# Reordering the end of layer 1: placing masks, products of blocks 6 and 7, chosen rows and block 7's scaling

## Chip, cores, metric

The kernel runs on one NeuronCore of a Trainium2 chip. The metric is device time in microseconds (us) of one execution; lower is better. A core has five engines that run side by side, each working through its own queue in program order: PE (TensorE, matrix products and transposes), VectorE (DVE in the profile), ScalarE (ACT), GpSimd (POOL) and SyncE (SP, which issues transfers). An engine stops at an instruction whose input isn't there yet, and all that stands behind it in the same queue waits too.

## What is computed

Four layers, each an attention part and a feed-forward part on a residual x, 4096 tokens of 128 values in fp32. The change is in the feed-forward part of the second layer (layer 1 in the code):

```
def _ln(x, g, b):
    mu = jnp.mean(x, axis=-1, keepdims=True)
    var = jnp.mean(jnp.square(x - mu), axis=-1, keepdims=True)
    return (x - mu) * jax.lax.rsqrt(var + EPS) * g + b
...
x1 = jnp.einsum('btd,hd->bth', x, sw1) + sb1
x2 = jnp.einsum('btd,hd->bth', x, sw2) + sb2
sh = _ln(jax.nn.silu(x1) * x2, s_ln_g, s_ln_b)
shared_out = jnp.einsum('bth,dh->btd', sh, sw3) + sb3
x_moe = x[index_b, index_t]
shared_scores = jax.nn.sigmoid(x_moe @ sg_w.T + sg_b)
expert_scores = jax.nn.sigmoid(x_moe @ eg_w.T + eg_b)
top1_idx = jnp.argmax(expert_scores + exp_bias, axis=-1)
...
shared_moe_out = shared_out[index_b, index_t] * shared_w[:, None]
h1 = jnp.einsum('md,ehd->meh', x_moe, ew1) + eb1
h2 = jnp.einsum('md,ehd->meh', x_moe, ew2) + eb2
z = _ln(jax.nn.silu(h1) * h2, sel_ln_g, sel_ln_b)
...
final_out = shared_out.at[index_b, index_t].set(shared_moe_out + expert_moe_out)
```

Every token takes a shared path with 64 hidden values. 256 chosen tokens take one of eight experts as well, and their result replaces that of the shared path. The input of both is the layer-normed residual, and the result is added to the residual. What follows is layer 2's attention, which starts with a norm of the new residual.

## The kernel before

**Blocks.** The 4096 tokens are eight blocks of 512 (`TB`), each held as four tiles of 128 tokens by 128 values (`x[b]`, `J` = 4). The order of the work is written out by hand (`tc.manual_schedule`): the instructions of each engine stand in the order of the calls. Layer 1 runs a loop of stages over the blocks with fixed lags, and then a list of calls for what remains of the last blocks: that list is what the change edits.

**A block's shared path.** `f_stats`, `f_scale` and `f_turn` norm a block, write its rows to DRAM (`by_rows`, issued by SP) and transpose it. `f_product(b)` makes the 128 products per token on PE and starts a tanh on ScalarE; the function it leaves in `t[b]["gated"]` makes silu times product on VectorE (L916, L919). `z_stats` takes mean and variance on VectorE (L715, L717, L718), with the inverse root on GpSimd (L242, L243, L720). `z_scale` scales four tiles of 128x64 on ScalarE (L726), `z_turn` transposes them on PE and evicts on ScalarE (L946) into one of two buffers `zts`. `z_out` makes the output product and adds it on VectorE (L790); `z_out_by_three` has ScalarE scale it (L970) and GpSimd add it (L973), the addition being returned to be called later (`add2`, `add3`, ...).

**The chosen rows.** `chosen_rows` gathers 256 rows from `by_rows` by two indirect transfers of GpSimd (L987), which need all row writes landed. `chosen_products` transposes them (L995), and makes gates, both hidden layers of all experts and the shared products; `chosen_gates` finds the expert; `chosen_select` and `chosen_shared` make z for the chosen expert and for the shared path; `chosen_norm` and `chosen_scale` norm it (znc, L726); `chosen_mix` makes the weights (L1071 to L1081); `chosen_affine`, `chosen_turn`, `chosen_shared_out`, `chosen_products_out` and `chosen_out` make the 256 result rows `val`. For block 0 they are put in by a product with 0/1 masks: `put_rows` makes the masks on GpSimd (L772), `chosen_put_product` multiplies, `chosen_put` adds to `x[0]`. For the other blocks `chosen_back` writes the rows to DRAM (`back`, L1151), whence layer 2 fetches them.

**The end.** Block 0's new residual is normed (`stats_of`, `scaled`), transposed (L748), and evicted (L750) as layer 2's first `xt`. Layer 2's first steps are `qb` on VectorE (L2086), the products for q and k on PE, and q's eviction with `qb` on ScalarE (L1441). `keep_clock(4)` before the last transposes makes four products of the unit matrix with itself whose result isn't used.

Of the kernel before, what the change touches and what calls it, by code (L numbers as in the profile page):

```python
# [160 lines left out]
def body(ctx, tc, dram, spans, x_in, ib, it, ic, ei, out):  # L161
# [23 lines left out]
    def bank(tag="one"):  # L185
        if tag == "one" and "own" in banks:
            return banks["own"]
        return banks["pool"].tile([P, TB], F32, tag=tag, name="ps1", bufs=banks["tags"][tag])
# [579 lines left out]
    def put_rows(b, pool, engine, tag=None):  # L768

        put = pool.tile([P, 4 if tag else 2, TB], F32, tag=tag or "put", name="put")  # L770
        for m in range(2):
            engine.tensor_scalar(  # L772
                put[:, m, :], c["iota512"], float(b * TB), at_col[:, m : m + 1], ALU.add, ALU.is_equal
            )
        return put

    def keep_clock(n):

        ps = bank()
        for _ in range(n):  # L780
            mm(cols(ps, 0), ident, ident)
# [12 lines left out]
    def layer1():  # L794
# [9 lines left out]
        with tc.tile_pool(name="l1", bufs=2) as wp, tc.tile_pool(name="l1c", bufs=1) as once:  # L804
# [102 lines left out]
            def f_turn(b):  # L907
                t[b]["fxt"] = turned(wp, "fxt", t[b]["fxn"], 5)
# [22 lines left out]
            def f_gate(b):  # L931
                f_product(b)
                t[b]["gated"]()

            def z_stats(b):
                t[b]["zby"] = stats_of(t[b]["z"], J)

            def z_scale(b):
                t[b]["zn"] = wp.tile([P, J, 64], F32, tag="zn", name="zn")
                scaled(t[b]["zn"], t[b]["z"], t[b]["zby"], J)  # L940

            def z_turned(zn, i, n):
                ps = bank()
                for j in range(n):
                    nc.tensor.transpose(ps[:64, j * P : (j + 1) * P], zn[:, j, :], ident)
                nc.scalar.activation(  # L946
                    zts[i][:64, : n * P],
                    ps[:64, : n * P],
                    AF.Identity,
                    bias=l1["slb"][:64],  # L950
                    scale=l1["slg"][:64],
                )

            def z_turn(b):
                z_turned(t[b]["zn"], b % 2, J)

            def z_out(b):
                zt = zts[b % 2]
# [3 lines left out]
            def z_out_by_three(b):  # L962


                zt = zts[b % 2]
                pv = by_token([(lambda j: cols(zt, j), l1["sw3"][:65])], None)
                zo = wp.tile([P, J, D], F32, tag="zo", name="zo")
                for j in range(J):
                    k = b * J + j
                    nc.scalar.activation(  # L970
                        zo[:, j, :], pv[:, j, :], AF.Identity, scale=rest[:, k : k + 1]
                    )
                return lambda: nc.gpsimd.tensor_tensor(x[b], x[b], zo, ALU.add)  # L973
# [73 lines left out]
            def chosen_shared():  # L1047
                c_["gated"]()
# [14 lines left out]
            def chosen_norm():  # L1063

                c_["by"] = stats_of(c_["zs"], 4)
# [17 lines left out]
            def chosen_scale():  # L1083
                c_["zn"] = zn = once.tile([P, 4, 64], F32, tag="znc", name="znc")
                scaled(zn, c_["zs"], c_["by"], 4)
# [8 lines left out]
                        (ALU.mult, ALU.add)[k],  # L1094
                    )

            def chosen_turn():
                zn = c_["zn"]
                z_turned(zn[:, 2:, :], 2, 2)
                pts = c_["pts"] = []  # L1100
                for m in range(2):
                    ze = wp.tile([P, 8, 64], F32, tag="ze", name="ze")
                    nc.vector.tensor_tensor(
                        ze,
                        zn[:, m, :].unsqueeze(1).to_broadcast([P, 8, 64]),
                        c_["pick"][:, m, :].unsqueeze(2).to_broadcast([P, 8, 64]),
                        ALU.mult,
                    )
                    pt = bank()
                    zf = ze.rearrange("p (i e) h -> p i (e h)", i=4)  # L1110
                    for i in range(4):
                        nc.tensor.transpose(cols(pt, i), zf[:, i, :], ident)
                    zte = wp.tile([P, TB], F32, tag="zte", name="zte")
                    (nc.vector.tensor_copy if m else nc.scalar.copy)(zte, pt)
                    pts.append(zte)
# [39 lines left out]
            def chosen_put_product():  # L1155
                c_["pv"] = put_product(c_["put"])
# [26 lines left out]
            with tc.manual_schedule():  # L1183

                nc.scalar.activation(
                    stat.tile([P, J], F32, tag="nb", name="nb")[:, :1], half[:, :1], AF.Exp
                )
                for zt in zts:
                    nc.gpsimd.memset(zt[64:65, :], 1.0)
                nc.gpsimd.memset(top_row, 0.0)  # L1190
                nc.gpsimd.memset(top_row[:1, :], 1.0)
                for k, name in enumerate(("eb1", "eb2")):
                    lo, hi = spans["rows"][name]
                    nc.sync.dma_start(ebs[:, k, :], dram["rows"][:, lo:hi].partition_broadcast(P))
                nought = once.tile([P, J, D], F32, tag="nought", name="nought")
                nc.gpsimd.memset(nought, 0.0)
                for b in range(1, NB):
                    nc.sync.dma_start(
                        back[b * TB : (b + 1) * TB, :].rearrange("(j p) d -> p j d", p=P), nought
                    )  # L1200
                for i in range(NB):
                    for f, lag in stages:
                        if 0 <= i + lag < NB and (f, i) != (turn_, 0):
                            f(i + lag)


                gather(7)
                f_stats(5)
                output(6)
                z_scale(1)  # L1210
                attend(7)
                f_stats(6)
                f_gate(2)
                turn_o(7)
                f_scale(5)
                z_turn(1)
                output(7)
                f_stats(7)
                f_scale(6)
                f_turn(5)  # L1220
                f_scale(7)
                z_out(1)
                z_stats(2)
                c_["put"] = put_rows(0, wp, nc.gpsimd)
                chosen_rows()
                chosen_biases()
                f_turn(6)
                f_gate(3)
                z_scale(2)
                z_stats(3)  # L1230
                f_turn(7)
                z_turn(2)
                f_gate(4)
                z_stats(4)
                chosen_products()
                chosen_gates()
                z_scale(3)
                add2 = z_out_by_three(2)
                f_product(5)
                chosen_select()  # L1240
                z_turn(3)
                add3 = z_out_by_three(3)
                chosen_shared()
                chosen_norm()
                add2()
                z_scale(4)
                z_turn(4)
                add3()
                chosen_scale()
                t[5]["gated"]()  # L1250
                z_stats(5)
                chosen_mix()
                add4 = z_out_by_three(4)
                f_product(6)
                chosen_affine()
                chosen_turn()
                add4()
                chosen_shared_out()
                t[6]["gated"]()
                chosen_products_out()  # L1260
                z_stats(6)
                z_scale(5)
                z_turn(5)
                f_product(7)
                chosen_out()
                chosen_put_product()
                z_scale(6)
                add5 = z_out_by_three(5)
                t[7]["gated"]()
                z_stats(7)  # L1270
                chosen_put()

                by = stats_of(x[0], J)
                chosen_back()
                add5()
                z_turn(6)
                z_scale(7)
                z_out(6)
                z_turn(7)
                xn = norm.tile([P, J, D], F32, tag="xn", name="xn")  # L1280
                scaled(xn, x[0], by, J)
                nc.gpsimd.tensor_tensor(
                    x[0], x[0], bc["lb"].unsqueeze(1).to_broadcast([P, J, D]), ALU.add
                )
                z_out(7)
                keep_clock(4)
                t[0]["next"] = turned(norm, "xt", xn)


    I3 = 352  # L1290
# [861 lines left out]
```

## Time and profile before

| | us |
|---|---|
| runs of the kernel | 1476.65, 1475.78, 1473.11 (median 1475.78) |
| profiled execution | 1477.4, of which span 1475.6 |
| PE busy | 1396.4 (95% of the span) |
| VectorE busy | 982.0 (67%) |
| ScalarE busy | 1047.2 (71%) |
| GpSimd busy | 652.3 (44%) |

"Busy" is the time in which an engine had an instruction under way. The list that the change edits covers some 480 to 533 us of the span, that is 3.6% of it. To read this stretch one needs the views by time: the chain of waits (the work that ended last, followed back from the end, here in order of time), the timeline of single instructions (start, length, engine, line, operation, output<-inputs, and in brackets how long the engine had been idle and what ended that), and the table of stretches (busy time of each engine and the TensorE clock that was granted, 1.00 being full speed).

| chosen steps before | starts at, us |
|---|---|
| first gather of chosen rows (GpSimd, L987) | 486.08 |
| scaling of the chosen rows' z (ScalarE, znc) | 507.85 |
| its transposes (PE, L945 on znc) | 513.84 |
| product with the masks (PE, val and put) | 520.61 |
| norm of block 0: scaling (ScalarE, xn) | 527.69 |
| eviction of layer 2's first xt (ScalarE, L750) | 532.51 |
| first q of layer 2 (ScalarE, L1441) | 536.97 |

### The profile page before, as it was taken

Reading aid. Unit: us, or ns where it says so; the run is one execution under the profiler, and the core shown is the slowest. Engines: PE = TensorE matmul, PEld = TensorE weight load, DVE = VectorE, ACT = ScalarE, POOL = GpSimd, SP = SyncE. Lnnn points to the kernel's source line nnn. Section 1 sums busy time; section 2 is a strip of 40 time slices with the busy share of each in tenths; the row PEclk is TensorE's granted clock in tenths of the full one; section 3 lists DMA queues with packets and bytes.
Section 4 is the critical chain, followed back from the end, with each engine's and each line's share of the span. In section 5 each row is a group of like instructions: output and inputs, shape, how many; then the busy total and the mean of one; then the engine's idle time right before and its main releaser. Section 6 shows DMA issues by size and latency. Waiting matters only on the chain.

```text
span 1475.6 us, 22195 instructions
## 1 busy us (share of the span) xinstructions
PE 1396.4 (95%) x7716; PEld 670.2 (45%) x7716; DVE 982.0 (67%) x2050; ACT 1047.2 (71%) x2140; POOL 652.3 (44%) x749
## 2 busy tenths in 40 slices
PE   7789999999889889999999999999999999999997
PEld 3652222222367554443443445444445454454465
DVE  6776665675377558642673487786786777877876
ACT  7869999999777556664865585876876867668632
POOL 6647666665555533310530172452442623524423
PEclk9999999999899889999999999999999999999998
DMA  4039999898431010101000000000000000000000
GB/s 170 1 54 132 134 129 130 129 128 114 103 132 30 18 40 24 36 3 29 1 1 1 1 1 8 1 1 8 1 1 8 1 8 1 1 8 1 1 8 15
DMA packets 33233, 59.42 MB, mean 40 GB/s; under 512 B 5602, under 2 KB 25634, under 8 KB 28643
## 3 DMA queue, kind: packets, MB, share of 16 engines
q1 hardware_dynamic: 32416, 56.18, 21.9%
q8 instruction: 61, 1.00, 0.3%
q10 hardware_dynamic: 578, 1.57, 0.3%
q14 instruction: 50, 0.40, 0.1%
q0 software_dynamic: 128, 0.26, 0.0%
HBM read 49.70 MB, written 8.29 MB: 39 GB/s over the span
## 4 chain that ended last, share of the span: by engine, by line
PE 69%; ACT 14%; DVE 9%; DMA 5%; issue 1%; POOL 1%; POOLq 0%; DVEq 0%; SPq 0%; ACTq 0%
PE ps L246 66%; ACT hm L563 6%; DMA gs<-gates 4%; ACT hm L562 3%; ACT ex L1469 2%; DMA gates<-eq 1%; DVE s L715 1%; DVE nm L1463 1%; ACT xn L1385 1%; PE ps L1799 1%; ACT xn L726 1%; POOL rs L243 0%; DVE pr L575 0%; ACT h L384 0%; DVE x L270 0%
## 5 line engine op out<-in xcount | busy, mean ns | idle before, releaser
L1469 ACT ACTIVATE ex<-ps,nm 128x512 f32<-128x512 f32 x512 | 346.3, 688 | 182.4 <-DVE nm L1463 176.3
L1463 DVE TENSOR_REDUCE nm<-ps 128x2 f32<-128x1024 f32 x256 | 300.5, 1216 | 61.3 <-PE ps L246 60.9
L246 PE MATMUL ps<-q,k 64*128 64x512 f32 x1024 | 256.9, 617 | 5.7 <-ACT ex L1469 4.9
L246 PE MATMUL ps<-ex,vs 128*64 128x512 f32 x1024 | 233.8, 598 | 0.0
L581 POOL TENSOR_TENSOR acc<-acc,pr 128x512 f32<-128x512 f32 x119 | 166.6, 1400 | 107.9 <-DVE pr L575 99.7
L1484 POOL TENSOR_TENSOR vs<-v,sm 128x256 f32<-128x256 f32 x128 | 81.4, 636 | 296.7 <-DVE sm L1483 267.6
L563 ACT ACTIVATE hm<-ps,blob_f 128x1536 f32<-128x1536 f32 x128 | 196.4, 1535 | 0.0
L246 PE MATMUL ps<-xt,blob_a 128*128 128x512 f32 x304 | 152.3, 627 | 0.7 <-ACT xt L750 0.7
L575 DVE SCALAR_TENSOR_TENSOR pr<-ps,blob_f,gs 128x512 f32<-128x512 f32 x120 | 90.1, 751 | 91.0 <-PE ps L246 74.6
L246 PE MATMUL ps<-h,w 32*128 32x512 f32 x1024 | 148.0, 639 | 2.3 <-ACT xt L750 0.8
L246 PEld LDWEIGHTS ps<-q,k 64*128 64x128 f32 x1024 | 87.0, 185 | 137.5 <-issue 69.9
L246 PE MATMUL ps<-hm,w 128*32 128x512 f32 x1024 | 137.1, 607 | 4.5 <-DVE pr L575 3.8
L246 PEld LDWEIGHTS ps<-ex,vs 128*64 128x64 f32 x1024 | 67.8, 136 | 148.5 <-issue 130.8
L1671 POOL TENSOR_TENSOR acs<-acs,prod 128x512 f32<-128x512 f32 x98 | 124.7, 1273 | 10.7 <-ACT prod L1670 6.3
L242 POOL TENSOR_SCALAR rs<-mv 128x4 f32<-128x4 f32 (+1 forms) x69 | 18.1, 262 | 201.8 <-DVE mv L1375 140.7
L1469 ACT ACTIVATION_READ_ACCUMULATOR ex<-ps,nm 128x1 f32 x512 | 104.7, 205 | 0.0
L562 ACT ACTIVATE hm<-ps,blob_f 128x512 f32<-128x512 f32 x128 | 88.2, 689 | 18.1 <-PE ps L246 18.0
L246 PEld LDWEIGHTS ps<-xt,blob_a 128*128 128x128 f32 x304 | 53.0, 193 | 88.6 <-issue 62.6
L246 PEld LDWEIGHTS ps<-h,w 32*128 32x128 f32 x1024 | 40.9, 183 | 110.3 <-ACT hm L562 93.7
L1431 DVE TENSOR_TENSOR v<-ps,blob_bc 128x512 f32<-128x512 f32 x64 | 44.2, 691 | 67.7 <-PE ps L246 43.2
L246 PEld LDWEIGHTS ps<-blob_a,ct 128*128 128x128 f32 x512 | 67.0, 191 | 32.3 <-issue 29.2
L243 POOL TENSOR_TENSOR rs<-rs,half 128x4 f32<-128x4 f32 (+1 forms) x69 | 72.4, 1049 | 5.8
(301 smaller groups left out, 2206.6 us busy)
## 6 DMA issues: line engine op xcount, KB each, us to landing
gs<-gates SPq DMA_DIRECT2D x256, 128.0 KB
blob_f<-in_f SPq DMA_DIRECT2D x1, 2560.0 KB
blob_a<-in_a SPq DMA_DIRECT2D x1, 2056.0 KB
x<-in_x SPq DMA_DIRECT2D x8, 256.0 KB
gates<-eq SPq DMA_DIRECT2D x8, 256.0 KB
ge<-gates SPq DMA_DIRECT2D x4, 512.0 KB
back<-nought SPq DMA_DIRECT2D x7, 256.0 KB
by_rows<-fxn SPq DMA_DIRECT2D x7, 256.0 KB
```

The lines of the kernel that those rows point to most:

```text
L242: nc.gpsimd.tensor_scalar(t, var, EPS, None, ALU.add)
L243: nc.gpsimd.tensor_tensor(t, t, half[:, : t.shape[-1]], ALU.pow)
L246: nc.tensor.matmul(out_, lhs, rhs, start=start, stop=stop)
L562: nc.scalar.activation(hm[:, 0, :], p1, AF.Gelu, bias=bias)
L563: nc.scalar.activation(hm[:, 1:, :], p3, AF.Gelu, bias=bias)
L575: nc.vector.scalar_tensor_tensor(pr, po, f0["b2"][:, e : e + 1], gs, ALU.add, ALU.mult)
L581: nc.gpsimd.tensor_tensor(acc[:, b, :], acc[:, b, :], pr, ALU.add)
L1431: nc.vector.tensor_tensor(v, pv, bias, ALU.add)
L1463: nc.vector.tensor_reduce(nm, ps, AX.X, ALU.max, negate=True)
L1469: nc.scalar.activation(ex[kt][:, i, :], ps[:, i, :], AF.Exp, bias=nm[:, i : i + 1], accum_out=sm[:, kt, i : i + 1],)
L1484: nc.gpsimd.tensor_tensor(vs[:, tiles, :, :], vs_[n][:, tiles, :].rearrange("p j (i n) -> p j i n", i=2), sm[:, tiles, :].unsqueeze(3).to_ ...
L1671: nc.gpsimd.tensor_tensor(t["acs"], t["acs"], p, ALU.add)
```

## The change

- `put_rows` makes its two masks on VectorE instead of GpSimd.
- `z_scale(2)` comes before `f_gate(3)`.
- After the norm of the chosen rows, `f_product(6)` and `f_product(7)` come early, beside the mix, and block 4's scaling, transposes and output come later, between the steps of the chosen rows.
- `chosen_turn` is split: spreading z over the eight experts (`chosen_spread`, VectorE) is called before block 6's gate.
- Block 7's scaling is done by VectorE (`z_scale_by_vector`), and so is the eviction of its transposes; blocks 5, 6 and 7 are added by `z_out` on VectorE, blocks 2, 3 and 4 by GpSimd.
- `chosen_back` comes after block 0's scaling; block 0 is transposed before block 7's output; `keep_clock(4)` is left out.

```diff
+            def z_scale_by_vector(b):
+                t[b]["zn"] = zn = wp.tile([P, J, 64], F32, tag="zn", name="zn")
+                nb, rs = t[b]["zby"]
+                for j in range(J):
+                    nc.vector.tensor_scalar(
+                        zn[:, j, :], t[b]["z"][:, j, :], rs[:, j : j + 1], nb[:, j : j + 1],
+                        ALU.mult, ALU.add,
+                    )
...
-            def z_turned(zn, i, n):
+            def z_turned(zn, i, n, by_vector=False):
                 ps = bank()
                 for j in range(n):
                     nc.tensor.transpose(ps[:64, j * P : (j + 1) * P], zn[:, j, :], ident)
+                if by_vector:
+                    nc.vector.tensor_scalar(
+                        zts[i][:64, : n * P], ps[:64, : n * P], l1["slg"][:64], l1["slb"][:64],
+                        ALU.mult, ALU.add,
+                    )
+                    return
...
-            def chosen_turn():
+            def chosen_spread():
                 zn = c_["zn"]
-                z_turned(zn[:, 2:, :], 2, 2)
-                pts = c_["pts"] = []
                 for m in range(2):
-                    ze = wp.tile([P, 8, 64], F32, tag="ze", name="ze")
+                    c_["ze", m] = ze = wp.tile([P, 8, 64], F32, tag="ze", name="ze")
                     nc.vector.tensor_tensor(
...
+            def chosen_turn():
+                z_turned(c_["zn"][:, 2:, :], 2, 2)
+                pts = c_["pts"] = []
+                for m in range(2):
                     pt = bank()
-                    zf = ze.rearrange("p (i e) h -> p i (e h)", i=4)
+                    zf = c_["ze", m].rearrange("p (i e) h -> p i (e h)", i=4)
...
-                c_["put"] = put_rows(0, wp, nc.gpsimd)
+                c_["put"] = put_rows(0, wp, nc.vector)
                 chosen_rows()
                 chosen_biases()
                 f_turn(6)
+                z_scale(2)
                 f_gate(3)
-                z_scale(2)
...
                 chosen_shared()
+                add2()
                 chosen_norm()
-                add2()
-                z_scale(4)
-                z_turn(4)
-                add3()
                 chosen_scale()
+                f_product(6)
                 t[5]["gated"]()
                 z_stats(5)
                 chosen_mix()
-                add4 = z_out_by_three(4)
-                f_product(6)
+                f_product(7)
                 chosen_affine()
+                chosen_spread()
+                t[6]["gated"]()
                 chosen_turn()
-                add4()
+                add3()
                 chosen_shared_out()
-                t[6]["gated"]()
+                z_scale(4)
+                t[7]["gated"]()
+                z_stats(6)
                 chosen_products_out()
-                z_stats(6)
+                z_turn(4)
                 z_scale(5)
-                z_turn(5)
-                f_product(7)
                 chosen_out()
                 chosen_put_product()
+                z_stats(7)
                 z_scale(6)
-                add5 = z_out_by_three(5)
-                t[7]["gated"]()
-                z_stats(7)
+                add4 = z_out_by_three(4)
+                z_turn(5)
                 chosen_put()
 
                 by = stats_of(x[0], J)
-                chosen_back()
-                add5()
                 z_turn(6)
-                z_scale(7)
-                z_out(6)
-                z_turn(7)
+                z_scale_by_vector(7)
+                z_out(5)
+                z_turn(7, True)
                 xn = norm.tile([P, J, D], F32, tag="xn", name="xn")
                 scaled(xn, x[0], by, J)
+                chosen_back()
+                add4()
+                z_out(6)
+                t[0]["next"] = turned(norm, "xt", xn)
                 nc.gpsimd.tensor_tensor(
                     x[0], x[0], bc["lb"].unsqueeze(1).to_broadcast([P, J, D]), ALU.add
                 )
                 z_out(7)
-                keep_clock(4)
-                t[0]["next"] = turned(norm, "xt", xn)
```

More of the change, by code (lines that the diff above doesn't have):

```diff
@@ L952, in z_turned, with z_turn @@
                 )
-            def z_turn(b):
-                z_turned(t[b]["zn"], b % 2, J)
+            def z_turn(b, by_vector=False):
+                z_turned(t[b]["zn"], b % 2, J, by_vector)
             def z_out(b):
```

## The prediction

> **What bounds the kernel now.** The page says that PE is busy for 95% of the span, and its chain puts 69% on PE. That is an average: layers 0 and 2 are long runs of products. The change sits between 480 and 537 us, so I read that stretch alone: first the chain of waits, in order of time.
>
> ```profile
> 486.08 1.23 POOL row L987
> 487.61 2.40 DMA row<-by_rows,at_int
> ...
> 490.99 7.30 PE ps L246 x14
> ...
> 506.96 1.16 DVE mix L1072
> ...
> 508.96 5.04 PE ps L246 x18
> ...
> 527.84 3.79 PE ps L246 x16
> 531.62 0.87 PE ps L748 x4
> ...
> 533.15 3.80 PE ps L246 x4
> ```
>
> (start, length, what.) Until 490 the chain hangs on the gather of the chosen rows. Then it goes through ScalarE, VectorE and GpSimd one after another, and three times through PE at a length that its work doesn't explain: the last line is four 128x512 products, which take 1.88 at 540.62. The stretches of that view show why:
>
> ```profile
> core 0: us, PE busy (x) PEld busy (x) DVE busy (x) ACT busy (x) POOL busy (x), PEclk, DMA share, GB/s
> 486.47:489.89 3.42, 1.46 (x6) 0.47 (x4) 1.73 (x10) 0.60 (x2) 3.00 (x4) 1.00 0.11 38
> 489.89:496.71 6.82, 6.19 (x12) 3.46 (x13) 2.51 (x16) 0.97 (x3) 1.75 (x5) 0.50 0.00 0
> 503.53:506.95 3.42, 1.77 (x11) 0.97 (x9) 3.28 (x19) 2.46 (x8) 2.77 (x5) 1.00 0.00 0
> 506.95:513.78 6.83, 5.59 (x21) 4.22 (x21) 3.21 (x7) 3.50 (x10) 4.19 (x5) 0.50 0.00 0
> 524.02:527.43 3.41, 1.63 (x12) 1.33 (x12) 2.46 (x15) 3.02 (x9) 2.20 (x6) 1.00 0.01 2
> 527.43:537.67 10.24, 8.42 (x24) 5.41 (x24) 2.84 (x7) 3.18 (x7) 4.51 (x4) 0.50 0.37 121
> 500.13:503.54 3.41, 2.54 (x17) 1.72 (x16) 3.18 (x10) 2.87 (x9) 1.04 (x1) 1.00 0.00 0
> ```
>
> The granted clock is 0.50 in three stretches of 2, 2 and 3 times 3.41 us, and their starts are 5 and 6 times 3.41 apart: the clock is decided on a grid of 3.41 us. Each slow stretch follows a grid step in which PE was busy for 1.46, 1.77 or 1.63; after 2.54 it stayed up. The third thing is queues: these lines of the timeline stand in front of work that was ready.
>
> ```profile
> 505.32 1.44 ACT L726 ACTIVATE zn<-z,nb,rs 128x64 f32<-128x64 f32 x4
> 507.17 0.78 ACT L946 ACTIVATE zt<-ps,blob_l 64x512 f32<-64x512 f32 x1 [0.41 <-PE ps L945]
> 507.85 1.43 ACT L726 ACTIVATE znc<-zs,nb,rs 128x64 f32<-128x64 f32 x4
> ...
> 505.79 1.10 DVE L718 TENSOR_SCALAR nb<-mv 128x4 f32<-128x4 f32 x1
> ...
> 529.71 1.92 PE L246 MATMUL ps<-blob_c 128*128 128x128 f32 x8
> ```
>
> The chosen rows' scaling (znc) had its statistics at 505.64 and began at 507.85, behind block 4's. A 128x4 VectorE operation took 1.10 instead of 0.17, ending with GpSimd's addition. The last line is the clock-keeping products, in front of block 0's transposes.
>
> **The change, part by part**, in times of this trace.
>
> *Masks by VectorE.* GpSimd loses 2 x 2.01 (481.88 to 485.89), all of it ahead of the gather. VectorE gains two 128x512 tensor_scalars: between 0.36 (128x384, L1321) and 0.75 (128x512 from PSUM, L1442) each; I take 0.5, so 1.0, which lies in VectorE's idle 3.82 before 484.23 and costs nothing. The gather can't start at 481.9: it waits for block 7's last row write (issued at 481.6, landing 2.4 to 2.7 later), so at about 484.4 instead of 486.08. **-1.6**; at least 0 if a straggling write lands late. Block 2's scaling moves ahead of block 3's tanh on ScalarE (both short of work there: 0).
>
> *Clock at the chosen rows' products.* PE now runs out at about 486.4 instead of 487.62 (block 2's scaling, moved ahead, frees the transposes that idled PE for some 1.0 from 484.57), turns two rows, and starts products at 489.4. The Trainium skill, "TensorE: Matmul & The Clock Gate", last table, asks for no idle gaps over about 3 us. My gap is 2.2 us, so by that rule the clock stays and the 4.2 us of products at half speed shrink by another 3.2. By the row it falls: 1.46 of 3.42 busy, with no idle of 3 us in it, was enough, and I expect no more than that here. I take the row: **0**, between -3.2 and 0.
>
> *Chosen rows first.* From the end of the second tanh (498.9 before, 497.3 after): two select operations 1.4, GpSimd 1.05, reduction 1.05, shared z 0.56, statistics 1.1, GpSimd 1.5, so znc starts 6.8 later, at 504.0, against 8.9 before; the 2.2 behind block 4 goes. VectorE's 1.10 and 1.16 for nb and mix go with add3, which now comes after the norm; add2 runs before it. Then PE: before, 4.6 passed from the end of znc (509.28) to its transposes (513.84), filled by block 4's output and block 6's products at half clock (1.91 + 3.5). Now block 6's products (1.8 at full clock) lie beside the norm, where PE had nothing, and only block 7's 1.8 stand between pick (505.0) and the transposes: 507.3. **-6.5 in all** at this point, of which 1.6 is the gather. It needs full clock from 496.7 on; if that falls, 1.8 comes back.
>
> *Spread, and products of 7 taken out of the tail.* From the transposes to the product with the masks: 6.77 before, with block 7's product (1.75) between. Now about 5.1, ended by val (VectorE 0.42), beside block 4's transposes: 512.4. Its evacuation to block 0 waited for VectorE until 523.24, 2.63 after the product; block 7's statistics are now done before, so 2.0: block 0 is updated from 514.4. **-8.8.**
>
> *Block 0's norm.* Statistics to GpSimd's nb take 3.9 (523.24 to 527.2) as before: 518.4. The scaling then waited 0.5 for ScalarE behind blocks 6 and 7; block 7's scaling and eviction are now on VectorE (4 x 128x64: between 0.17 of a 128x4 and 0.34 of a 128x128 from PSUM, I take 0.2 apart; eviction 0.75 by L1442, against ScalarE's 0.78). Its transposes waited until 531.41 for block 7's output and four keep-clock products (2.08 + 1.92 at half clock); now they follow the scaling piece by piece: xt at 520.7 against 532.51. **-11.8.** Block 5's addition goes from GpSimd (1.29) to VectorE (1.12), which then has, from 516.9: scaling 0.8, additions of block 5 1.1, eviction 0.7, additions of 6 and 7 2.2; with PE's products between them it is through at about 522.6, before GpSimd, so it decides nothing. Behind them stands block 7's output, 0.9 on PE, before layer 2's first product.
>
> *What is late next.* The first q needs qb, a VectorE operation, and L2086 was held by GpSimd's addition (0.73 for 128x8). The Trainium skill, "GPSIMD Engine Reference", section 1, says that GpSimd shares its SBUF interface with VectorE's two-port instructions; the trace agrees (1.10, 1.16, 0.73). GpSimd now has, after 518.4: 1.1 + 1.5 + 1.0 for the two write-backs, 1.3 for block 4, 1.3 for block 0's bias: 524.6. PE alone would allow q at 523.4. So q at 524.7 against 536.97: **-12.3**; without the hold -13.6. From there layer 2 follows in the same order (rows of back and weights on SP come as much earlier as the write-backs do).
>
> *Clock at layer 2's start.* PE waits 2 us there for q, and the four keep-clock products are gone. A grid step under 1.8 busy is about as likely as not, and two slow steps of products cost up to 3.4: **+1.7**, between 0 and 3.4. Sum: **-10.6**.
>
> The profiled execution took 1477.4 (span 1475.6 and 1.8 around it): 1466.8. It is the slowest of the four times; the median less 10.6 is 1465.2. I forecast **1465.5**.
>
> **Rivals.**
> 1. *The clock stays up at the chosen rows* (their gap splits over two grid steps): a further -3.2 and most of the 1.7: 1461. For it: 500.13 to 503.54 with 2.54 busy stayed up. Against: some 3 us of near idleness cover most of any step. 0.16.
> 2. *Layer 2 starts at half clock and stays there* for five or six steps instead of two: its first frames wait on VectorE and ScalarE, and in this trace it took three steps to come back. 17 to 20 us at half speed cost 8 to 10 in place of 1.7: 1472 to 1475. 0.12, half of it within 0.3%.
> 3. *Slower*: the same mechanism decides the other way only if the slow clock outlasts 10 steps (34 us, 17 lost against 12.3 + 4.4), 521 to 555. Against it: the trace was back at 537.67 although it had also started low. With it I count a GpSimd queue that holds VectorE's scaling and qb beyond what I see. About 1481. 0.06.
> 4. *Not what it says*: the order of the built instructions has moved as the diff says, but a row write landing 1.6 late leaves the gather where it was: 1467; inside the forecast.
> The forecast itself has 0.66, with 1461 to 1470 as its own range.
>
> **Numbers.** 0.3% (4.4 us) is about what a measurement here can tell. Below 1471.4: 0.66 + 0.16 + a third of rival 2, less a tail: 0.86; within: 0.08; above 1480.2: 0.06. Range 1459 to 1473: rival 1 whole, and half of rival 2.
>
> **What the new profile should show.** The gather's issue at 484 to 485; znc straight after nb, 6.8 after the second tanh; block 7's product, not block 4's output, ahead of the chosen transposes; no 0.50 around 507 to 514; xt near 521; qb ending just after GpSimd's last addition and q right behind it. I am wrong if the clock is 0.50 in more than four or five grid steps, or if q comes later than 530.

## The result, and the profile after

The changed kernel takes 1464.93 us (median of six runs, 1463.46 to 1466.74); the kernel before, run beside it, takes 1475.01 (1473.11 to 1477.86). The ratio is 0.993, with a 95% interval from 0.9916 to 0.9945: 10.1 us, or 0.7%, faster. The forecast was 1465.5, with -10.6 as the sum of its steps.

The profiled execution took 1466.0 (span 1464.2), 11.4 less than that of before. Not all of this belongs to the change. The scaling of block 7's rows, which comes just ahead of the edited list, began at 479.66 before and at 478.54 after: 1.1 us of the difference lies ahead. At layer 1's start the clock was at 0.50 in three stretches in the execution of before, and in one in that of after. I therefore count from the start of that scaling.

| us after the start of block 7's row scaling | before | after | difference | the prediction's running sum |
|---|---|---|---|---|
| first gather issued (GpSimd) | 6.42 | 5.91 | -0.5 | -1.6 |
| second tanh of the chosen rows ends | 19.25 | 18.67 | -0.6 | -1.6 |
| scaling of the chosen rows' z (znc) | 28.19 | 25.36 | -2.8 | -3.8 |
| its transposes | 34.18 | 28.11 | -6.1 | -6.5 |
| product with the masks | 40.95 | 33.37 | -7.6 | -8.2 |
| block 0 updated from that product | 43.58 | 35.46 | -8.1 | -8.8 |
| norm of block 0: scaling (xn) | 48.03 | 39.47 | -8.6 | -9.3 |
| eviction of layer 2's first xt | 52.85 | 42.72 | -10.1 | -11.8 |
| first q of layer 2 | 57.31 | 47.51 | -9.8 | -12.3 |
| last (64th) q of layer 2 | 907.01 | 897.09 | -9.9 | -10.6 |

(The prediction put the clock's loss of 1.7 behind the first q: hence -12.3 there and -10.6 later.) The last two rows say that what was won in the stretch is kept: 850 us later layer 2 is as far ahead as at its first q.

First the chain of waits of the changed kernel over the stretch, in order of time (start, length, what):

```profile
484.45 0.54 POOL row L1002
484.99 0.99 issue
485.98 2.51 DMA row<-by_rows,at_int
...
489.48 7.11 PE ps L246 x14
...
504.68 0.38 PE ps L1094 x2
505.06 1.75 PE ps L246 x10
506.81 0.22 PE ps L954 x2
...
518.75 1.62 PE ps L246 x8
520.37 0.85 PE ps L748 x4
521.22 4.80 PE ps L246 x12
526.05 0.70 ACT q L1458
```

Until 497 it is the old chain: gather, transposes, 7.11 us of products at half speed. In the middle VectorE's 1.16 for mix is gone, and the products that stand between the pick (L1094) and the chosen transposes (L954) are block 7's, 1.75 us at full speed. The end is a run of PE work from 518.75 to q: there PE is the limit, and at half speed.

The timeline shows the same at single instructions (start, length, engine, line, operation, output<-inputs, and in brackets the idle time before and what ended it):

```profile
484.45 1.23 POOL L1002 DMA_INDIRECT row<-by_rows,at_int  x1 [3.61 <-DMA by_rows<-fxn]
503.90 1.43 ACT L726 ACTIVATE znc<-zs,nb,rs 128x64 f32<-128x64 f32 x4 [0.16 <-POOL nb L720]
504.08 0.17 DVE L718 TENSOR_SCALAR nb<-mv 128x4 f32<-128x4 f32 x1
...
522.72 3.29 PE L246 MATMUL ps<-xt,blob_a 128*128 128x512 f32 x4
524.28 0.17 DVE L2103 TENSOR_SCALAR qb<-blob_a 128x8 f32<-128x8 f32 x1 [0.19 <-POOL x L1301]
526.05 0.69 ACT L1458 ACTIVATE q<-ps,qb 128x512 f32<-128x512 f32 x1 [4.21 <-PE ps L246]
```

The gather now waits for the last row write (3.61 us of idle GpSimd), not for masks. The scaling znc follows its statistics after 0.16 us. And qb is there at 524.45, but q starts at 526.05, when PE is through with the first four products: they took 3.29 us, where 1.88 is their time at full clock. The stretches tell why (columns as in the table of before: the clock is the one ahead of the DMA share):

```profile
core 0: us, PE busy (x) PEld busy (x) DVE busy (x) ACT busy (x) POOL busy (x), PEclk, DMA share, GB/s
484.59:488.00 3.41, 0.98 (x3) 0.14 (x1) 2.41 (x17) 0.38 (x1) 3.00 (x4) 1.00 0.15 38
488.00:494.83 6.83, 5.83 (x12) 3.40 (x13) 2.34 (x15) 0.60 (x3) 1.99 (x5) 0.50 0.00 0
505.07:508.48 3.41, 3.39 (x25) 2.60 (x25) 2.59 (x6) 2.41 (x8) 2.63 (x3) 1.00 0.00 0
515.31:518.72 3.41, 2.03 (x18) 1.72 (x17) 2.33 (x15) 3.17 (x9) 2.05 (x4) 1.00 0.00 0
518.72:525.55 6.83, 6.83 (x25) 5.01 (x23) 4.64 (x14) 1.52 (x4) 3.99 (x4) 0.50 0.18 56
```

Of the three slow stretches the middle one is gone (505 to 508 is nearly full of PE work), the one at the chosen rows has stayed, and the one at layer 2's start has become shorter, two grid steps instead of three. In both kernels it begins about where block 0's scaling xn does: at 527.43 with xn at 527.69 before, at 518.72 with xn at 518.01 after.

### The profile page after: what moved, and what is told of

It is laid out like the page before. It is cut to its first block, busy times and chain, and to the rows that moved or that the text cites. A ratio compares the mean times of both kernels' runs of the same rounds, so it can differ in the third digit from the quotient of the medians.

```text
span 1464.2 us, 22177 instructions
## 1 busy us (share of the span) xinstructions
PE 1387.7 (95%) x7708; PEld 665.4 (45%) x7708; DVE 982.4 (67%) x2061; ACT 1042.7 (71%) x2131; POOL 647.3 (44%) x746
## 3 DMA queue, kind: packets, MB, share of 16 engines
q10 hardware_dynamic: 578, 1.57, 0.3%
## 4 chain that ended last, share of the span: by engine, by line
PE 68%; ACT 13%; DVE 9%; DMA 6%; issue 2%; POOL 1%; SPq 0%; POOLq 0%; DVEq 0%; ACTq 0%
PE ps L246 66%; DMA gs<-gates 5%; ACT hm L563 5%; ACT ex L1486 2%; ACT hm L562 2%; DVE nm L1480 1%; DVE s L715 1%; DMA gates<-eq 1%; ACT xn L1402 1%; PE ps L1816 1%; DVE x L270 1%; ACT xn L726 1%; POOL rs L243 0%; ACT h L384 0%; SPq L543 0%
```

## The experiments

The main theory is that of the prediction: the order of the queues and the clock that follows from it give the 10 us, most of it between the second tanh and the mask product. The rival readings: that the clock alone made it (an order is worth little, PE must only be kept busy), that the masks made it, or that the end after block 0's norm made it. The runs are told by question. "Kept" means that products of the unit matrix with itself, whose result isn't used, are put where PE was idle.

**How much is the middle?** The changed kernel, with the calls between the chosen norm and the mask product in the order of before (the addition of block 4, which the change had put behind xn, moves back with them):

```diff
                 chosen_shared()
-                add2()
                 chosen_norm()
+                add2()
+                z_scale(4)
+                z_turn(4)
+                add3()
                 chosen_scale()
-                f_product(6)
                 t[5]["gated"]()
                 z_stats(5)
                 chosen_mix()
-                f_product(7)
+                add4 = z_out_by_three(4)
+                f_product(6)
...
```

> The changed kernel with the calls from the shared gate to the product with the masks in the order of before (products of blocks 6 and 7, block 4's steps), everything ahead of and behind it as changed. Theory (the middle is the change's largest part): from the second tanh of the chosen rows to the product with the masks 14.7 us pass in the changed kernel and 21.7 in the kernel before; the 7.0 come back, with a stretch at 0.50 in the middle of it: 1472. Rival (the gain is made at the end, by block 0's norm, and the middle only moves waits): 1467 or less.

Measured: 1477.26 (1473.43 to 1479.63), ratio to before 1.0006 (0.9993 to 1.0019). The whole gain is gone, more than was expected. Its chain of waits:

```profile
504.45 1.10 DVE nb L718
505.62 1.16 DVE mix L1087
507.04 0.59 PE ps L1094 x2
507.63 4.97 PE ps L246 x18
...
530.97 3.77 PE ps L246 x4
534.76 0.70 ACT q L1458
535.55 6.77 PE ps L246 x20
```

VectorE's 1.10 and 1.16 are back, and so is the middle slow stretch (505.5 to 512.3): 4.97 us of products stand between the pick and the transposes, where the changed kernel has 1.75. The mask product comes 6.7 us later than in the changed kernel. From there to xt this kernel needs 8.8 us (before: 11.9), so the changed end does win 3 here, and at xt this kernel is 3.9 ahead of the kernel before. But layer 2 starts with four grid steps at 0.50 (526.0 to 539.6): the lead is 1.7 at the first q, and at the second it is gone (the twenty products between take 6.77, against 4.81 in the changed kernel).

**How much is the end?** The changed kernel up to block 0's norm, then calls in the manner of before (block 5 added by GpSimd, block 7 scaled and evicted by ScalarE, its output and four clock-keeping products ahead of block 0's transposes):

```diff
                 by = stats_of(x[0], J)
+                chosen_back()
+                add4()
+                add5 = z_out_by_three(5)
+                add5()
                 z_turn(6)
-                z_scale_by_vector(7)
-                z_out(5)
-                z_turn(7, True)
+                z_scale(7)
+                z_out(6)
+                z_turn(7)
                 xn = norm.tile([P, J, D], F32, tag="xn", name="xn")
                 scaled(xn, x[0], by, J)
...
```

> The changed kernel up to the norm of block 0, and from there the order of before: write-backs first, block 5 by GpSimd, block 7 scaled and evicted by ScalarE, its output and four unit-matrix products ahead of block 0's transposes. Theory (terms add up): from the product with the masks to xt 11.9 us pass in the kernel before and 9.35 in the changed one; 2.2 to 2.6 come back, 1467.3. Rival (the middle decides all, as the run with the middle of before gave back everything): 1465.

Measured: 1472.11 (1469.55 to 1475.43), ratio 0.9973 (0.9963 to 0.9984), so some 6 us of the gain are gone, more than twice what was expected. The mask product and then ScalarE in the timeline of this kernel:

```profile
512.12 2.05 PE L246 MATMUL ps<-val,put 128*128 128x128 f32 x16
...
518.56 1.14 ACT L985 ACTIVATE zo<-ps,rest 128x128 f32<-128x128 f32 x4 [1.25 <-PE ps L246]
519.57 0.77 ACT L961 ACTIVATE zt<-ps,blob_l 64x512 f32<-64x512 f32 x1
520.23 1.43 ACT L726 ACTIVATE zn<-z,nb,rs 128x64 f32<-128x64 f32 x4
523.37 0.77 ACT L961 ACTIVATE zt<-ps,blob_l 64x512 f32<-64x512 f32 x1 [1.70 <-PE ps L954]
524.04 1.64 ACT L726 ACTIVATE xn<-x,nb,rs 128x128 f32<-128x128 f32 x4
```

Block 0's scaling xn stands behind four steps of blocks 5, 6 and 7 in one queue, and behind PE's half-speed work for them (the clock is at 0.50 from 518.5): 11.9 us after the mask product, in the changed kernel 6.1. But in the kernel before it was 7.1: this run isn't the old end on its own. The changed middle leaves more work behind: when block 0 is updated (514.2), ScalarE still has block 4's output and block 5's eviction to do (515.5 to 517.3), which the kernel before has done by then, and after them the four steps above. From the mask product to xt this run needs 16.8 us, the kernel before 11.9. So it shows that the end has to fit the middle, and not what the old end costs.

Taking back the middle thus costs 11 us (0.993 against 1.0006), and this other end 6 (0.993 against 0.9973). Together that is 17, and the change gives 10: the parts don't add. The first half loses its lead to four slow grid steps at layer 2's start, which the changed kernel, with two, doesn't have. The second loses 6.0 us at xn already, by the work in front of it and by half-speed products, and reaches q 5.5 later.

**Is it the clock alone?** The kernel before, its order untouched, with kept clock at six places:

```diff
+                    keep_in(ps[:, 256:], (8, 3)[m])
...
-                add3 = z_out_by_three(3)
+                add3 = z_out_by_three(3, 3)
...
-                z_turn(4)
+                z_turn(4, 6)
...
-                add4 = z_out_by_three(4)
+                add4 = z_out_by_three(4, 2)
...
-                z_out(6)
+                z_out(6, 6)
...
-                z_out(7)
+                z_out(7, 3)
```

(`keep_in(ps, n)` is n products of the unit matrix with itself into a bank that the next step overwrites; the last argument of the others passes such an n. The first line stands ahead of each transpose of gathered rows.)

> The kernel before, its order unchanged, with unit-matrix products where PE waits (8 and 3 ahead of the chosen rows' transposes, 3 to 6 ahead of the outputs of blocks 3, 4, 6 and 7 and of block 4's transposes), each in the bank that the next step writes. If the clock is what the change won: the three stretches at 0.50 with 20.2 us of PE work at half speed go, up to 10.1 us less, 1466 to 1468. If the order is what it won: the chain runs through the other engines and the added products stand in PE's way; 3 us less at most, 1472.5 or more. Both in part, as the terms of the prediction have it (some 4 of its 12 us are products at half speed): 1470 to 1472.

Measured: 1470.66 (1468.01 to 1472.86), ratio 0.9956 (0.9943 to 0.9968), some 6 us faster than before with no reordering. In its profile one grid step at 0.50 is left in the stretch (506.1 to 509.5), and its first q comes at 51.1 on the scale of the table: 6.2 ahead of before, 3.5 behind the changed kernel. Where the two win is not the same. The end of the second tanh and the mask product in this profile:

```profile
495.48 0.60 ACT L1021 ACTIVATE se<-ps 128x512 f32<-128x512 f32 x1 [1.12 <-PE ps L246]
517.35 1.95 PE L246 MATMUL ps<-val,put 128*128 128x128 f32 x16
```

| stretch, us | before | clock kept | changed |
|---|---|---|---|
| row scaling to second tanh's end | 19.25 | 16.50 | 18.67 |
| from there to the mask product | 21.70 | 21.27 | 14.70 |
| from there to the first q | 16.36 | 13.29 | 14.14 |

The middle, where the change wins 7.0 us, gains 0.4 from kept clock, though one slow step is left in it: that part is order. At the end kept clock alone wins more than the change does (3.1 against 2.2), and 2.7 come from the chosen rows, where the changed kernel is still slow.

**Would the clock at the two places left in the changed kernel be worth something?** First at the chosen rows: eight unit products ahead of the first row's transpose, three ahead of the second's.

```diff
                 for m in range(2):
+                    keep_in(ps[:, 256:], (8, 3)[m])
```

> The changed kernel with eight unit-matrix products ahead of the first transpose of the chosen rows and three ahead of the second, in unused columns of the same PSUM bank, where PE waits for the gather. Theory (the clock follows how long PE was busy in a grid step of 3.41 us): the granted clock stays 1.00 over the chosen rows' products; of the 5.35 us at half speed there (489.48 to 494.83) 2.7 go: 1462.2, about 12.8 below the kernel before. Rival (only idle gaps beyond 3 us lower the clock, or these products don't count): the stretch at 0.50 stays and the time is that of the changed kernel, 1464.9.

Measured: 1465.49 (1464.09 to 1467.84), ratio 0.9935 (0.992 to 0.9949): nothing to be seen in the time. The stretches of this kernel:

```profile
core 0: us, PE busy (x) PEld busy (x) DVE busy (x) ACT busy (x) POOL busy (x), PEclk, DMA share, GB/s
487.43:490.84 3.41, 2.60 (x14) 1.75 (x13) 0.51 (x3) 0.56 (x2) 2.26 (x5) 0.99 0.03 10
490.84:494.25 3.41, 3.41 (x5) 1.33 (x4) 2.50 (x14) 0.60 (x1) 0.00 (x0) 0.51 0.00 0
494.25:497.67 3.42, 3.42 (x24) 2.82 (x23) 2.34 (x5) 2.02 (x7) 1.22 (x2) 1.00 0.00 0
```

One slow step is left instead of two, so neither expectation holds whole. (The run with the masks on GpSimd, below, has one step there too, without these products.) The clock fell at 490.84 although PE had been busy for 2.60 of the 3.41 us before.

Then at layer 2's start: five unit products ahead of block 5's output product.

```diff
-                z_out(5)
+                z_out(5, 5)
```

> The changed kernel with five unit-matrix products ahead of block 5's output product, in the same bank, where PE was idle for 1.38 us. Theory: the stretch at 0.50 from 518.7 to 525.6 goes, but q then waits for qb behind GpSimd's addition of block 0's bias (524.45): 1.5 gained at q, and PE, idle for 2 us there, falls to half speed one grid step later and gives back 0 to 3.4: 1463.4 to 1466.8. Rival (qb doesn't hold q, PE alone does): 2.7 gained, 1462.2.

Measured: 1464.69 (1463.27 to 1466.8), ratio 0.993 (0.9915 to 0.9944). Its q starts 2.0 us earlier on the scale of the table (45.5), and now right behind qb. But then PE has nothing to do: two lines of this kernel, the first of its timeline, the second of its stretches.

```profile
523.68 3.17 PE L246 MATMUL ps<-q,k 64*128 64x512 f32 x8 [2.01 <-ACT q L1463]
```

```profile
core 0: us, PE busy (x) PEld busy (x) DVE busy (x) ACT busy (x) POOL busy (x), PEclk, DMA share, GB/s
520.93:524.34 3.41, 1.40 (x6) 0.43 (x6) 1.56 (x3) 0.69 (x1) 1.89 (x2) 1.00 0.39 116
```

PE waits 2.01 us for q, the step has 1.40 us of work, and the next step is at 0.50. At the second q the lead has shrunk from 2.0 to 0.4 us (52.7 against 53.1), and 0.4 ahead is where this execution was at the second tanh already.

Both together, with GpSimd's addition of block 0's bias moved behind the first queries of layer 2:

> All three edits together. Theory: 2.7 + 2.7 below the changed kernel, 1459.5, 15.5 below the kernel before. Rival (the chain behind the chosen rows' products is bound by other engines, or the slow stretch only moves to a later grid step): 1462 or more.

Measured: 1463.04 (1462.04 to 1466.37), ratio 0.9921 (0.9905 to 0.9936). This is the fastest median of all; its interval overlaps that of the changed kernel, so it isn't shown to beat it, and the 1459.5 of the theory isn't reached. In its profile the stretch has no slow step at all, and its first and its last q of layer 2 come 4.2 us earlier than in the changed kernel. The medians show 1.9 of it and the profiled executions 2.9 (1463.1 against 1466.0). Of the rest 1.1 lies ahead of anything that was edited: this profile has three slow stretches at layer 1's start, as before has, and that of the changed kernel has one, so that the row scaling begins 1.1 later. And 2.5 of the 4.2 are won ahead of the second tanh, by the same products at the chosen rows that left one slow step in the run with them alone: what they do to the clock differs between executions.

**What does q wait for when PE is early?** In the run with products at layer 2's start it was qb on VectorE, which the prediction had put behind GpSimd's additions. Moving the bias addition alone, on top of the products at layer 2's start (`nc.gpsimd.tensor_tensor(x[0], ...)` to behind `queries(0)`):

> The same with GpSimd's addition of block 0's bias moved behind layer 2's first query, so that qb is no longer held by it. Theory: qb at about 523.2, q right behind it, no 0.50 at the start of layer 2: 2.7 below the changed kernel, 1462.2. Rival (qb's hold costs nothing): the same time as the run before it.

Measured: 1465.91 (1465.36 to 1467.5), ratio 0.9938 (0.9924 to 0.9951), q at 46.0: no gain. GpSimd has nothing else to do at the first queries, so the addition still followed block 4's directly, and qb, beside it, took 0.73 us instead of 0.17. The next two runs do the opposite: both additions ahead of the write-backs `chosen_back`, with kept clock at both places, and alone:

```diff
                 scaled(xn, x[0], by, J)
-                chosen_back()
                 add4()
                 z_out(6)
                 t[0]["next"] = turned(norm, "xt", xn)
                 nc.gpsimd.tensor_tensor(
                     x[0], x[0], bc["lb"].unsqueeze(1).to_broadcast([P, J, D]), ALU.add
                 )
+                chosen_back()
                 z_out(7)
```

> The changed kernel with the unit-matrix products at the chosen rows and ahead of block 5's output, and with GpSimd's additions of block 4 and of block 0's bias ahead of its two write-backs instead of behind them. Theory (qb, and with it q, waits for GpSimd's additions behind the write-backs): qb ends some 2.3 us earlier after block 7's row scaling than with the products alone (43.2), q is then set by PE at about 41.7: 1.6 below the run with all kept, 1461.4. Rival (layer 2 needs the rows written back, which now come 2.5 later): 1463 or more.

> The changed kernel with those two additions ahead of the write-backs, and nothing else. Theory: where PE is at half speed at layer 2's start, as in the profile, q waits for PE and nothing is gained; where it isn't, q comes 1.6 earlier and PE has less idle time there: 1463.5 to 1465. Rival (GpSimd's queue always sets q): 1.6 in every run, 1463.3 or less.

Measured: 1468.36 (1464.25 to 1470.2), ratio 0.994 (0.992 to 0.9959), and 1466.96 (1465.54 to 1469.99), ratio 0.9939 (0.9921 to 0.9956). The theory that the additions hold qb fell. The timeline of the first of them:

```profile
523.61 0.96 POOL L1175 DMA_INDIRECT back<-val,at_int  x1 [1.53 <-DMA back<-val,at_int]
...
526.20 0.37 SPq L2090 DMA_DIRECT2D rows<-back  x1
...
526.41 0.17 DVE L2109 TENSOR_SCALAR qb<-blob_a 128x8 f32<-128x8 f32 x1 [4.06 <-issue]
526.66 0.69 ACT L1464 ACTIVATE q<-ps,qb 128x512 f32<-128x512 f32 x1 [6.17 <-DVE qb L2109]
```

VectorE had nothing to do for 4.06 us and GpSimd's additions were through at 520.8. What ended just before qb is the second write-back: SyncE, which fetches the rows that it wrote, goes on at 526.20, and qb follows at 526.41. In the built program qb, VectorE's first instruction of layer 2, stands behind waits for the transfers under way at that point, though its own inputs come from none of them; in this trace VectorE stands for 4.53 us at the one for the second write-back. This wait is not new in these two runs. In the run with the masks on GpSimd, whose end is that of the changed kernel and whose clock stayed up there, the same three steps read:

```profile
520.52 0.96 POOL L1169 DMA_INDIRECT back<-val,at_int  x1 [1.54 <-DMA back<-val,at_int]
523.31 0.72 DVE L2103 TENSOR_SCALAR qb<-blob_a 128x8 f32<-128x8 f32 x1 [1.08 <-POOL x L988]
524.12 0.69 ACT L1458 ACTIVATE q<-ps,qb 128x512 f32<-128x512 f32 x1 [3.72 <-DVE qb L2103]
```

From the issue of the second write-back to qb it is 2.79 us here and 2.80 above, and 2.78 to 2.80 in all eight profiles in which VectorE had been idle for 1 us or more ahead of qb, the kernel before among them. Where GpSimd adds a block's output right behind the write-back, the addition ends just as the transfer lands, and so the profile names the addition; the two runs that moved it tell the two apart. GpSimd's part is that qb then takes 0.72 instead of 0.17 us. So the write-backs have to be early. A version without that wait was not tried, so what it would give is open.

**The masks.** The changed kernel with the masks on GpSimd again (`put_rows(0, wp, nc.gpsimd)`):

> The changed kernel with its two masks made by GpSimd again, ahead of the gather. Reading of the two traces: the gather waits for the last row write, which landed 5.9 us after block 7's row scaling began; GpSimd would be through with the masks 6.3 after it. So the masks' part of the change is worth 0.4 us, and this kernel takes 1465.3. Rival (the prediction's term): 1.6 us, 1466.5, with the gather 1.6 later than in the changed kernel.

Measured: 1464.98 (1464.14 to 1466.06), ratio 0.9923 (0.9899 to 0.9948). Its timeline:

```profile
480.87 4.01 POOL L772 TENSOR_SCALAR put<-blob_c,at_col 128x512 f32<-128x512 f32 x2
485.11 1.23 POOL L1002 DMA_INDIRECT row<-by_rows,at_int  x1 [0.23 <-issue]
```

The masks are done at 484.88 and the gather follows 0.23 later: 6.45 us after the start of block 7's row scaling, against 5.91 (and 6.42 before). In the eleven profiles of kernels that have the masks on VectorE and the same work ahead of the gather this number lies between 5.26 and 6.39, as the last row write lands earlier or later. So taking the masks from GpSimd is worth some half a microsecond, from nothing to 1.2 in single executions. In this one it may have cost nothing: the last row write landed 5.62 after the scaling's start, and the gather came 0.83 behind that, as it does in all eleven.

**Block 7's scaling.** The changed kernel with `z_scale(7)` and `z_turn(7)`, both on ScalarE:

> The changed kernel with block 7's scaling and the eviction of its transposes on ScalarE, at the same places in the order. Theory (ScalarE's queue sets block 0's scaling): block 0's scaling starts behind that eviction, 1.6 us later (519.6 instead of 518.0), and xt and q follow: 1466.0 to 1466.5. Rival (PE at half speed sets xt there, and ScalarE has slack): the scaling is later by less than 0.5 and the time is that of the changed kernel, 1464.9.

Measured: 1466.55 (1465.0 to 1467.3), ratio 0.9933 (0.9909 to 0.9958). The profile agrees with the theory in place and sign: xn starts 8.4 us after the mask product instead of 6.1, of which 1.1 is left at xt and 0.5 at q. The median is where the theory put it, but in time the run can't be told from the changed kernel.

**The changed kernel again**, beside the last of these runs:

> The changed kernel once more, as the measure for the three runs beside it: 1464.9; between its runs the slow stretches of the clock lie elsewhere, so q comes 45.5 to 47.5 us after block 7's row scaling.

Measured: 1466.24 (1463.14 to 1468.55), ratio 0.9932 (0.9913 to 0.995). Its profile has the same two slow stretches of two steps each as the first one, and q at 47.8, just outside what was expected.

## Why the prediction was right, point by point

**The gather: -1.6 forecast, -0.5 measured.** The mechanism was right: the masks are gone, and the row write is what it waits for. The term was mis-sized in two ways. The write was taken to land at about 484.4, 4.7 us after the row scaling's start; it landed 5.1 after it (before: 5.0). And the gather was taken to start with the landing; in the changed kernel it starts 0.83 later (counted from the end of GpSimd's wait for that transfer), and so in every profile with masks on VectorE. In the kernel before, where the masks ended later than that, nothing of this could be seen. The fourth rival, a late write, is the smaller part. The loss of 1.1 us runs through every later row of the table.

**Clock at the chosen rows: 0 forecast, right.** The step with the gather had 0.98 us of PE work, and the two after it were at 0.50. The first rival, that the clock stays up there, didn't come about; its size was given wrongly, since 4.2 us of half-speed products can't shrink by 3.2, but the run with all kept, with the clock up, does need 2.7 us less from gather to second tanh. The prediction had set the rule of the Trainium skill (the page "TensorE: Matmul & The Clock Gate", last table: idle gaps of some 3 us) against a row of the trace and took the row. The runs go further in that direction: in the changed kernel the only gap of PE that the timeline shows between 509.8 and 526.0 is one of 1.38 us, ending at 517.15, and the clock was halved at 518.72; in the run with kept clock at the chosen rows no gap from 480 on was longer than 0.55, and it was halved at 490.84.

**From the tanh to znc: -2.2 forecast, -2.2 measured.** znc waited for its statistics and for nothing else, 6.7 us after the tanh (forecast 6.8). **To the transposes: -2.7 forecast, -3.2 measured**; block 7's 1.75 at full clock was all that stood between. **Through mask product and update to block 0's scaling: -2.8 forecast, -2.5 measured.** VectorE's new work was priced well: 0.48 for a mask (0.5), 0.98 for block 7's scaling (0.8), 0.79 for its eviction (0.75).

**From xn to the first q: -3.0 forecast, -1.2 measured.** This is the term that failed most. The prediction had PE at full clock here and q held by qb, and it put the clock's loss behind q, as half of 3.4 us, because PE would wait there. In the changed kernel the clock was lost before xt: PE's gap of 1.38 us lies in front of block 5's output, the outputs of blocks 6 and 7 ran at half speed among block 0's transposes, from xn to xt it took 3.2 us instead of 2.3, and the first four products took 1.4 more than at full clock. So q came 1.6 behind qb. That qb ended right behind GpSimd's last addition, as forecast, is a coincidence: in the changed kernel it stands behind VectorE's own addition of block 7, and where that was done early it waited for the second write-back, as shown above. The forecast path, q right behind qb, did come about in the run with the masks on GpSimd, where the clock stayed up: q at 45.5 after the row scaling, where 45.0 was forecast.

**Behind q: +1.7 forecast, -0.1 measured.** Nothing was lost there. The second rival, a layer 2 that stays at half speed for five or six steps, didn't come about either.

**The sum.** -9.8 at q against -12.3: by the second tanh 1.0 was missing, on the way from xn to q 1.7; the chosen transposes gave 0.5 more, and what lies between 0.3 less. That -10.6 was met is therefore partly luck: the loss of 1.7 that was forecast behind q didn't come and stood in for losses ahead of it. The middle, from the second tanh to the mask product, came out as reasoned: 7.0 us, where 6.6 were forecast.

## What to carry to other kernels

When a chain of short steps runs through several engines, let every step of the chain stand first in its queue and lay the independent products in the chain's gaps: here that bought time twice, by the wait itself and by a PE that stays at full clock. When you run half of a reordering, check that what it leaves in front of the part under test is what one of the two whole kernels has there: here one half had the leftovers of the changed kernel and the steps of the old one in front of the same norm, and the two halves cost 11 and 6 us of a whole of 10. And when a wait is removed, look at what else is awaited at the same place: behind PE stood qb, and behind qb a write-back that it has no use for.

## What the runs showed of the hardware

**PE's busy time doesn't settle the clock.** It was halved after steps of 3.41 us with 2.60 and 2.03 us of PE work, and it stayed at full after this one, in the kernel with kept clock at both places:

```profile
core 0: us, PE busy (x) PEld busy (x) DVE busy (x) ACT busy (x) POOL busy (x), PEclk, DMA share, GB/s
520.72:524.13 3.41, 1.56 (x5) 0.49 (x5) 1.80 (x4) 0.69 (x1) 2.12 (x2) 1.00 0.33 96
```

Here the 1.56 us are five matmuls, all 512 columns wide; the 2.60 hold fourteen, of which two are as wide and the others 128, 18 or 9 columns. That suggests that columns streamed count, and not time busy. But the step with 2.03 us in the changed kernel, eighteen products and transposes of 128 columns, has a twin in the run with the masks on GpSimd, with eighteen such products and nearly the same gap (1.36 us against 1.38), and there the clock stayed at full (the first line; columns as above):

```profile
514.49:517.91 3.42, 2.06 (x18) 1.79 (x17) 2.52 (x15) 3.11 (x9) 1.50 (x4) 1.00 0.00 0
517.91:521.32 3.41, 3.27 (x26) 2.82 (x25) 3.08 (x10) 2.07 (x5) 1.87 (x2) 1.00 0.05 19
```

The grid lies a little differently: the step ends 1.09 us after the gap here, and 1.57 after it in the changed kernel. So neither busy time nor gap nor columns of one step settle the clock, and what does stays open. Of the six profiles with the changed middle, block 5's output at this place and no products added to it, the clock fell there in five; of the four with five unit products ahead of that output, in none.

**What lies outside the edit moves the time as much as the edit.** The slow stretches at layer 1's start (one to three) and at the end of the kernel (5 to 13 us in all) differ between executions of kernels that are alike there. Runs of one kernel spread over 2 to 8 us, and the most that a further version won at q is 4.2; so the last few microseconds of this stretch are read from profiles, counted from a mark just ahead of the edit, and not from medians.
